# A decoder layer on Trainium2: the root of the FFN's inner layernorm by Newton's method on GpSimd

## The chip, the core and the metric

The kernel runs on one core of a Trainium2 chip. A core has five engines with a queue of instructions each: PE (TensorE, matrix products and transposes), DVE (VectorE), ACT (ScalarE, activation functions), POOL (GpSimd) and SP (SyncE, which issues transfers here). Each works through its queue in order; between engines semaphores say when data is there. The metric is the device time of one execution in microseconds (us).

## The reference

One decoder layer over x of 4 batches x 1024 tokens x 256 features: self-attention with 16 heads, cross-attention over 64 context tokens, and an FFN. Each of the three adds its result to x and begins with a layernorm. What the change touches is the FFN, which has a layernorm of its own between its two products:

```
h = einsum('btd,hd->bth', layernorm(x), absmean(W_fc))   # 256 -> 1024, weights -1, 0, 1
h = gelu(h)
mu  = mean(h);  var = mean((h - mu)**2)                    # over the 1024 values of a token
h = (h - mu) * rsqrt(var + 1e-5) * ln_w + ln_b
x = x + einsum('bth,dh->btd', h, absmean(W_proj))        # 1024 -> 256
```

The change is about `rsqrt(var + 1e-5)` and about when the line that uses it is issued.

## The kernel before

**Stages.** Self-attention of all four batches comes first and takes most of the time, with the cross-attention of each batch but the last woven into it. From about 1098 us on, the FFN of all batches runs, together with what is left of the last batch: its output projection, its cross-attention and the statistics of its last layernorm (the generator `post`, line 554; pieces of it are called the last batch's pieces). The tokens of a batch are worked in two halves of 512 tokens, so the FFN has 8 halves, called 0 to 7. A half has 4 tiles of 128 tokens.

**`widen(i)`** (line 1005) takes half i up. It normalises x into xn, transposes it on PE (L60), copies the transposes out of PSUM as xh on ACT (L279) and the rest xl on DVE (L281). Each tile is then multiplied by `wfc` (16 matmuls into one of the two buffers `ps_wide`); ACT applies Gelu (L1029); DVE takes the statistics of the 1024 values (two `bn_stats`, L1032, and an aggregation into `mvh`, L1033). When all four tiles have their statistics, `ln_rstd` (line 244) makes the reciprocal root of the variances, 128 x 4 values: Sqrt on ACT (L247), reciprocal on DVE (L248, `rsh`), and -mean x root on DVE (L1037, `nmr`). Then the tiles are normalised in place in two steps of two tiles: the even tile on DVE (L1040, needs `rsh`), the odd one on ACT (L1043, needs `nmr`).

**`narrow(i)`** (line 1048) takes half i down. For each of 8 blocks of 128 hidden features it transposes the four tiles (L60, into a bank of `ps_misc`), scales them by `ln_w` as hT on ACT (L1063), takes the rounding rest hl on DVE (L1064), and, two blocks behind, multiplies hl and hT by `wproj` on PE (L57). At the end DVE adds to x (L1082) and SP writes the rows out. `ps_misc` has four banks, which `narrow`, `widen` and the last batch share.

**Tables.** ACT holds one set of functions at a time. Sqrt, Gelu and Exp lie in different sets, so a change from one to another inserts an ACT_TABLE_LOAD in ACT's queue; copies and scalings need none.

**The order** is written out by hand, in pieces. `widen` and `narrow` are generators, and each `yield` ends a piece. Half i's `widen` has its pieces due at places 16 i + `WIDE`, its `narrow` at 16 (i + 1) + `NARROW`:

```
WIDE, NARROW = (-6, -4, 0, 1, 3, 7, 8, 10, 12), (2, 4, 5, 6, 9, 11, 13, 14, 15)
```

The loop after it (lines 1104 to 1130) always steps the piece with the smallest place among the first unfinished `widen` and the first unfinished `narrow`; in two turns of five it steps a piece of the last batch instead, as long as there are any. Of the nine places of `WIDE` the first two make xh and xl, those up to 7 end with the four tiles' matmuls and Gelus, 8 is the root, 10 and 12 are the two steps of normalisation. A condition named `apart` holds back a Gelu or Sqrt piece while the last batch is among its four Exp pieces. PE's instructions are kept in the order in which they are issued (`ordered`, line 56); on the other engines of this stage the framework's scheduler sets the order when the program is built, and it stays fixed from then on.

Of the kernel before, what the change touches and what calls it, by code (L numbers as in the profile page):

```python
# [8 lines left out]

F32 = mybir.dt.float32  # L10
F32R = mybir.dt.float32r
DRAM = bass.MemoryType.DRAM
AF = mybir.ActivationFunctionType
ALU = mybir.AluOpType
# [7 lines left out]
P = 128  # L22
NT = S // P
NG = 4
NU = B * NG
LN_EPS = 1e-5
# [4 lines left out]
def decoder_layer(ctx, tc, a, out):  # L31
# [15 lines left out]
    nc = tc.nc  # L47
# [8 lines left out]
    def matmul(*args, **kwargs):  # L56
        ordered(nc.tensor.matmul(*args, **kwargs))  # L57
# [44 lines left out]
    for name in ("wq", "wk"):  # L102
# [5 lines left out]
        t = const.tile([P, E // P, H, D], F32, name=name)  # L108
# [4 lines left out]
    for name in ("bq", "bk"):  # L113

        t = const.tile([P, 2], F32, name=f"{name}_c")
# [23 lines left out]
    kept_stack = ctx.enter_context(ExitStack())  # L139
    kept_pool = kept_stack.enter_context(tc.tile_pool(name="kept", bufs=1, space=DRAM))  # L140
    x_kept = kept_pool.tile([B * S, E], F32, name="x_kept").rearrange("(t p) d -> p t d", p=P)
# [7 lines left out]
    own = post_pool.tile([P, 4], F32, name="own")  # L149
    sel_x = post_pool.tile([P, 8, SK], F32R, name="sel_x")  # L150

# [3 lines left out]
    nc.gpsimd.memset(nm_s, 0.0)  # L155
    dram = main_stack.enter_context(tc.tile_pool(name="dram", bufs=1, space=DRAM))

# [3 lines left out]
    for i in range(3):  # L161
        t = (const if i else main).tile([P, NT, VW], F32, tag=f"v_sb{i}", name=f"v_sb{i}")
# [22 lines left out]
    def pinned(ins):  # L185

        if state["pinned"]:
            ordered(ins)
# [55 lines left out]
    def ln_rstd(pool, rs, mv):  # L244
        n = mv.shape[1]
        sd = pool.tile([P, n], F32, tag="sd", name="sd", bufs=2)
        nc.scalar.activation(sd, mv[:, :, 1], AF.Sqrt, bias=eps_t[:, 0:1])  # L247
        pinned(nc.vector.reciprocal(out=rs, in_=sd))  # L248

    def ln_normalised(pool, mv, rs, i, t, n):  # L250
        xn = pool.tile([P, n, E], F32, tag="xn", name="xn", bufs=2)
# [100 lines left out]
    def project(b, c):  # L352
# [6 lines left out]
        for side, half in ((0, 0), (1, 0), (1, 1), (0, 1)):  # L359
# [3 lines left out]
            for i0 in range(0, 512, width):  # L363
# [5 lines left out]
                )  # L369
                nc.scalar.activation(hl[:, 0, part].bitcast(F32R), pq, AF.Identity, bias=bias)  # L370
                nc.vector.scalar_tensor_tensor(  # L371
# [7 lines left out]
    def fetch(u):  # L379
# [4 lines left out]
        for pair in range(2):  # L384
            q = main.tile([P, S], F32R, tag="q", name="q", bufs=4)
            k = main.tile([P, S], F32R, tag="k", name="k", bufs=4)
            pairs.append((q, k))
# [66 lines left out]
    def turn_maxima(u, mx):  # L454
# [3 lines left out]
        dst = nm_s[:, :, :, 0:2, :]  # L458
        nc.vector.tensor_copy(dst[:, :, :, :, 0].bitcast(F32R), by_side)
        nc.vector.tensor_tensor(dst[:, :, :, :, 1], by_side, dst[:, :, :, :, 0], ALU.subtract)  # L460
        yield
        views = turned([nm_s[:, n, :, :, :].rearrange("p n a l -> p (n a l)") for n in range(4)])
        mT = main.tile([P, 512], F32R, tag="mT", name="mT", bufs=3)
        for r, v in enumerate(views):
# [447 lines left out]
    for u in range(NU):  # L912
# [27 lines left out]
        for step in range(2 * NT):  # L940
            half, kb = divmod(step, NT)
# [15 lines left out]
            exps = [scores(u, half, kb, 0)]  # L957
# [42 lines left out]
    ffn = ctx.enter_context(tc.tile_pool(name="ffn", bufs=1))  # L1000
    out_view = out.rearrange("(t p) d -> p t d", p=P)
    h_of = {}
    NH = NT // 2

    def widen(i):
        t0 = i * NH
        xh = ffn.tile([P, 2, NH * P], F32R, tag="xh", name="xh", bufs=2)
        xl = ffn.tile([P, 2, NH * P], F32R, tag="xl", name="xl", bufs=2)
        for t in range(0, NH, 2):
            cols = slice(t * P, (t + 2) * P)  # L1010
            xn = ln_normalised(ffn, mv3, rs3, t0 + t, t0 + t, 2)
            ln_transposed(xh[:, :, cols], xn, rest=xl[:, :, cols])
            if t == 0:
                yield ""
        h = ffn.tile([P, NH, HID], F32, tag="h", name="h", bufs=2)
        mv = ffn.tile([P, NH, 2], F32, tag="mvh", name="mvh", bufs=2)
        rs = ffn.tile([P, NH], F32, tag="rsh", name="rsh", bufs=2)
        h_of[i] = h
        for t in range(NH):
            yield "Gelu"  # L1020
            ph = ps["wide"]()
            for half in range(2):
                for k in range(4):
                    c, part = divmod(k, 2)
                    matmul(
                        ph[:, half, :], lhsT=(xl, xh)[part][:, c, t * P : (t + 1) * P],
                        rhs=wfc[:, c, half * 512 : (half + 1) * 512], start=k == 0, stop=k == 3,
                    )
            nc.scalar.activation(h[:, t, :], ph.rearrange("p a f -> p (a f)"), AF.Gelu)  # L1029
            st = ffn.tile([P, 2, 6], F32, tag="bnh", name="bnh", bufs=3)  # L1030
            for half in range(2):
                nc.vector.bn_stats(out=st[:, half, :], in_=h[:, t, half * 512 : (half + 1) * 512])  # L1032
            nc.vector.bn_aggr(out=mv[:, t, :], in_=st)  # L1033
        yield "Sqrt"
        ln_rstd(ffn, rs, mv)
        nmr = ffn.tile([P, NH], F32, tag="nmr", name="nmr", bufs=2)
        nc.vector.scalar_tensor_tensor(nmr, mv[:, :, 0], -1.0, rs, ALU.mult, ALU.mult)  # L1037
        for t in range(0, NH, 2):
            yield ""
            nc.vector.tensor_scalar(  # L1040
                h[:, t, :], h[:, t, :], mv[:, t, 0:1], rs[:, t : t + 1], ALU.subtract, ALU.mult
            )
            nc.scalar.activation(  # L1043
                h[:, t + 1, :], h[:, t + 1, :], AF.Identity, bias=nmr[:, t + 1 : t + 2],
                scale=rs[:, t + 1 : t + 2],
            )
# [57 lines left out]

    WIDE, NARROW = (-6, -4, 0, 1, 3, 7, 8, 10, 12), (2, 4, 5, 6, 9, 11, 13, 14, 15)
    halves = 2 * B
    wides = [Source(widen(i), 16 * i, WIDE) for i in range(halves)]
    narrows = [Source(narrow(i), 16 * (i + 1), NARROW) for i in range(halves)]  # L1110
    exps = turn = 0
    tag = later.tag
    while tag is not None or narrows:
        turn += 1
        if tag is not None and turn % 5 in (0, 2):
            exps += "Exp" in tag
            tag = next(last, None)
            continue
        sources = []
        if wides:  # L1120
            i = halves - len(wides)
            first = len(wides[0].places) <= len(WIDE) - 2
            late_x = i >= 2 * (B - 1) and tag is not None
            full = first and len(narrows) > halves + 1 - i
            apart = exps % NG and tag is not None and wides[0].tag in ("Gelu", "Sqrt")
            if not (late_x or full or apart):
                sources.append(wides[0])
        if narrows and len(narrows) > len(wides):
            sources.append(narrows[0])
        if not sources:  # L1130
            continue
        source = min(sources, key=lambda source: source.places[0])
        source.step()
        if not source:
            (wides if source in wides else narrows).pop(0)
# [58 lines left out]
```

## Time and profile before

| | |
|---|---|
| median of 3 runs | 1352.89 us (1351.7 to 1353.23) |
| the profiled execution | 1356.75 us |
| its span, first to last instruction | 1355.0 us |
| PE busy, share of the span | 1282.8 us, 95% |
| DVE / ACT / POOL busy | 1013.4 / 896.3 / 53.4 us |
| ACT_TABLE_LOADs from 1098 us on | 24 of 1.283 us each (12 ahead of Gelu, 9 ahead of Sqrt, 3 ahead of Exp) |
| Gelu activations L1029 | 32 of 1.025 us |
| normalisations L1040 on DVE / L1043 on ACT | 16 of 0.808 us / 16 of 1.236 us |
| hT L1063 on ACT / hl L1064 on DVE | 64 of 0.687 us / 64 of 0.734 us |

How to read the lines that follow. A line of the timeline has the start in us, the duration in us, the engine, the line of the kernel, the operation, output<-inputs, shapes and the count of instructions that were merged; brackets at its end give how long the engine sat idle before it and what ended that. A line of the waits says who waited for whom, with the total in us, the number of times and the longest. A line of the windows has the stretch and its length, then busy time and count for PE, PEld (weight loads), DVE, ACT and POOL, then PE's granted clock (1.00 is full speed), the DMA share and GB/s. Matmuls are pipelined: they start about 0.23 us apart (128x512) although each is shown longer.

### The profile page before, as it was taken

What the parts mean: (1) busy time and instruction counts of PE and PEld (TensorE: products, weight loads), DVE (VectorE), ACT (ScalarE), POOL (GpSimd) and SP (SyncE); (2) the same over time, 40 slices, a digit from 0 to 9 for tenths busy, and PEclk for the clock granted to TensorE, in tenths of its full rate; (3) what the DMA queues carried; (4) which work ended last, traced back from release to release, by engine and by line L of the source; (5) the groups of instructions that cost most, each with busy time, mean ns of one, the idle gap of its engine ahead of it and who ended that gap; (6) DMA issues with size and microseconds to landing.
All of it is one profiled execution on the core that took longest, in us unless ns stands there. A gap on an engine that the chain in (4) does not pass through costs nothing.

```text
span 1355.0 us, 27659 instructions
## 1 busy us (share of the span) xinstructions
PE 1282.8 (95%) x11000; PEld 719.0 (53%) x11000; DVE 1013.4 (75%) x2130; ACT 896.3 (66%) x1654; POOL 53.4 (4%) x66
## 2 busy tenths in 40 slices
PE   4889999999999999989999999999999999999987
PEld 2344545545545454444545544545455457776777
DVE  5777877867878888778777777778888468585765
ACT  1267686756687767677676676676766756575755
POOL 4000000003010000011000000010000000000000
PEclk9789999999999999999999999999999999999989
DMA  5440412212120202030202111312110010100000
GB/s 165 134 126 29 129 37 90 79 48 63 39 89 1 63 5 60 32 94 25 71 30 66 28 36 53 105 40 87 41 55 1 1 63 1 59 4 32 1 32 31
DMA packets 46576, 72.72 MB, mean 54 GB/s; under 512 B 11536, under 2 KB 28176, under 8 KB 46448
## 3 DMA queue, kind: packets, MB, share of 16 engines
q1 hardware_dynamic: 44976, 68.47, 16.8%
q10 hardware_dynamic: 1328, 2.10, 0.5%
q8 instruction: 87, 1.43, 0.4%
q0 software_dynamic: 144, 0.39, 0.2%
q14 instruction: 41, 0.34, 0.1%
HBM read 46.81 MB, written 24.12 MB: 52 GB/s over the span
## 4 chain that ended last, share of the span: by engine, by line
PE 74%; DVE 16%; ACT 7%; DMA 2%; issue 1%; SPq 0%; DVEq 0%; ACTq 0%
PE ps_ring L57 43%; PE ps_acc L57 15%; PE ps_wide L57 8%; DVE mx L447 7%; PE ps_misc L57 3%; DVE nm L603 3%; ACT exp L909 2%; PE ps_misc L60 2%; PE ps_ring L60 2%; ACT xn L258 1%; DVE bn L241 1%; DMA kept_k<-hl 1%; DMA x<-in_x 1%; ACT ex L636 1%; SPq L63 0%
## 5 line engine op out<-in xcount | busy, mean ns | idle before, releaser
L447 DVE TENSOR_REDUCE mx<-ps_ring 128x1 f32<-128x512 f32 x1024 | 646.9, 682 | 157.5 <-PE ps_ring L57 156.8
L909 ACT ACTIVATE exp<-ps_ring 128x512 f32<-128x512 f32 x1024 | 549.1, 607 | 182.1 <-PE ps_ring L57 178.7
L57 PE MATMUL ps_ring<-q,k 64*128 64x512 f32 x1024 | 280.4, 475 | 6.5 <-ACT exp L909 5.6
L57 PE MATMUL ps_ring<-k,q 64*128 64x512 f32 x1024 | 266.5, 428 | 18.2 <-DMA k<-kept_k 6.6
L57 PE MATMUL ps_acc<-exp,v_sb 128*32 128x512 f32 x2048 | 275.3, 610 | 0.0
L57 PE MATMUL ps_ring<-mT,sel 64*128 64x512 f32 x1024 | 233.4, 402 | 0.4 <-ACT mT L465 0.4
L57 PEld LDWEIGHTS ps_ring<-q,k 64*128 64x128 f32 x1024 | 115.8, 186 | 198.1 <-ACT exp L909 65.7
L57 PEld LDWEIGHTS ps_ring<-k,q 64*128 64x128 f32 x1024 | 127.0, 187 | 100.6 <-ACT exp L909 41.8
L57 PEld LDWEIGHTS ps_ring<-mT,sel 64*128 64x128 f32 x1024 | 108.7, 187 | 6.5 <-ACT mT L465 0.7
L57 PEld LDWEIGHTS ps_acc<-exp,v_sb 128*32 128x32 f32 x2048 | 40.5, 108 | 67.8 <-issue 66.0
L1064 DVE SCALAR_TENSOR_TENSOR hl<-ps_misc,lnw,hT 128x512 fp32r<-128x512 f32 x64 | 46.6, 734 | 20.0 <-ACT hT L1063 19.8
L1032 DVE BATCH_NORM_STATS2 bnh<-h 128x6 f32<-128x512 f32 x64 | 41.1, 680 | 24.7 <-ACT h L1029 24.6
L57 PE MATMUL ps_wide<-wfc,xl 128*128 128x512 f32 x128 | 55.6, 435 | 3.6 <-DVE xl L281 3.1
L1029 ACT ACTIVATE h<-ps_wide 128x1024 f32<-128x1024 f32 x32 | 32.7, 1025 | 36.8 <-PE ps_wide L57 36.7
L57 PE MATMUL ps_wide<-wproj,hl 128*128 128x256 f32 x256 | 46.8, 306 | 10.6 <-DVE hl L1064 10.5
L1063 ACT ACTIVATE hT<-ps_misc,lnw 128x512 fp32r<-128x512 f32 x64 | 42.9, 687 | 15.3 <-PE ps_misc L60 15.2
L57 PE MATMUL ps_wide<-wfc,xh 128*128 128x512 f32 x128 | 52.9, 413 | 0.0
L241 DVE BATCH_NORM_STATS2 bn<-x 128x6 f32<-128x256 f32 x96 | 39.0, 416 | 5.8 <-DMA x<-in_x 4.1
L57 PEld LDWEIGHTS ps_wide<-wproj,hl 128*128 128x128 f32 x256 | 35.3, 194 | 14.3 <-DVE hl L1064 12.6
L57 PE MATMUL ps_wide<-wproj,hT 128*128 128x256 f32 x256 | 42.0, 287 | 0.0
L371 DVE SCALAR_TENSOR_TENSOR hl<-ps_ring,bq_c,hl 128x256 f32<-128x256 f32 (+1 forms) x30 | 14.8, 500 | 31.0 <-ACT hl L370 31.0
L60 PE MATMUL ps_misc<-ident,h 128*128 128x128 f32 x256 | 37.3, 275 | 0.0
(167 smaller groups left out, 1424.0 us busy)
## 6 DMA issues: line engine op xcount, KB each, us to landing
q<-kept_q SPq DMA_DIRECT2D x240, 64.0 KB
k<-kept_k SPq DMA_DIRECT2D x240, 64.0 KB
kept_q<-hl SPq DMA_DIRECT2D x15, 512.0 KB
kept_k<-hl SPq DMA_DIRECT2D x14, 512.0 KB
out<-x SPq DMA_DIRECT2D x16, 256.0 KB
x<-in_x SPq DMA_DIRECT2D x3, 1024.0 KB
x_kept<-x SPq DMA_DIRECT2D x3, 1024.0 KB
x<-x_kept SPq DMA_DIRECT2D x3, 1024.0 KB
```

What stands on the lines that cost most here:

```text
L57: ordered(nc.tensor.matmul(*args, **kwargs))
L60: ordered(nc.tensor.transpose(*args))
L241: pinned(nc.vector.bn_stats(out=st, in_=xs(t)[:, 0, :]))
L258: nc.scalar.activation(xn[:, k, :], xs(t + k)[:, 0, :], AF.Identity, bias=nmr[:, k : k + 1], scale=rs[:, i + k : i + k + 1],)
L371: nc.vector.scalar_tensor_tensor(hl[:, 1, part], pq, bias, hl[:, 0, part], ALU.add, ALU.subtract)
L447: nc.vector.tensor_reduce(mx[:, t, 2 * pair + n : 2 * pair + n + 1, kh], pm, AX.X, ALU.max)
L603: nc.vector.tensor_reduce(nm[:, t, s, :], pm[s].rearrange("p (h k) -> p h k", k=SK), AX.X, ALU.max, negate=True,)
L909: nc.scalar.activation(ex[:, n, :], pe[n], AF.Exp)
L1029: nc.scalar.activation(h[:, t, :], ph.rearrange("p a f -> p (a f)"), AF.Gelu)
L1032: nc.vector.bn_stats(out=st[:, half, :], in_=h[:, t, half * 512 : (half + 1) * 512])
L1063: nc.scalar.activation(hT, pt, AF.Copy, scale=w)
L1064: nc.vector.scalar_tensor_tensor(hl, pt, w, hT.bitcast(F32), ALU.mult, ALU.subtract)
```

## The change

The Sqrt on ACT, the reciprocal and `nmr` on DVE give way to a function `ln_root` that makes both on GpSimd: variance + epsilon, a first guess from the bits of the number, three rounds of Newton's method, and -mean x root, 17 instructions on 128 x 4 values. The root no longer has a piece of its own: it is issued at the end of the piece of the fourth Gelu. The two steps of normalisation move from places 10 and 12 to 12 and 13, one place of `narrow` moves from 13 to 8, the last batch gets 7 turns of 17 instead of 2 of 5, and the condition `apart` names Gelu alone. The layernorms outside `widen` keep `ln_rstd`.

```diff
+    def ln_root(pool, rs, mv):
+        n = mv.shape[1]
+        by = pool.tile([P, 4, n], F32, tag="root", name="root", bufs=2)
+        var, half, t, nmr = (by[:, i, :] for i in range(4))
+        engine = nc.gpsimd
+        engine.tensor_scalar(var, mv[:, :, 1], LN_EPS, None, ALU.add)
+        engine.tensor_scalar(half, var, -0.5, None, ALU.mult)
+        engine.tensor_scalar(
+            rs.bitcast(I32), var.bitcast(I32), -0.5, float(0x5F3759DF), ALU.mult, ALU.add
+        )
+        for _ in range(3):
+            engine.tensor_tensor(t, rs, half, ALU.mult)
+            engine.tensor_tensor(t, t, rs, ALU.mult)
+            engine.tensor_scalar(t, t, 1.5, None, ALU.add)
+            engine.tensor_tensor(rs, rs, t, ALU.mult)
+        engine.tensor_tensor(nmr, mv[:, :, 0], rs, ALU.mult)
+        engine.tensor_scalar(nmr, nmr, -1.0, None, ALU.mult)
+        return nmr
...
-        yield "Sqrt"
-        ln_rstd(ffn, rs, mv)
-        nmr = ffn.tile([P, NH], F32, tag="nmr", name="nmr", bufs=2)
-        nc.vector.scalar_tensor_tensor(nmr, mv[:, :, 0], -1.0, rs, ALU.mult, ALU.mult)
+        nmr = ln_root(ffn, rs, mv)
...
-    WIDE, NARROW = (-6, -4, 0, 1, 3, 7, 8, 10, 12), (2, 4, 5, 6, 9, 11, 13, 14, 15)
+    WIDE, NARROW = (-6, -4, 0, 1, 3, 7, 12, 13), (2, 4, 5, 6, 8, 9, 11, 14, 15)
...
-        if tag is not None and turn % 5 in (0, 2):
+        if tag is not None and turn % 17 in (0, 2, 5, 7, 10, 12, 15):
...
-            apart = exps % NG and tag is not None and wides[0].tag in ("Gelu", "Sqrt")
+            apart = exps % NG and tag is not None and wides[0].tag == "Gelu"
```

## The prediction

> **What bounds the kernel now.** I read the page first. PE is the busiest engine, but a busy PE is not a fast one, so I went on to the stage that the change touches, the FFN (1098 us to the end), and asked for the waits in it, then for the timeline around each of its eight halves (called half 0 to half 7), then for the granted clock in slices of 3 us.
>
> ```profile
> PE 1282.8 (95%) x11000; PEld 719.0 (53%) x11000; DVE 1013.4 (75%) x2130; ACT 896.3 (66%) x1654; POOL 53.4 (4%) x66
> ```
> ```profile
> PEld ps_wide L57 <- DVE hl L1064: 12.6, 9, 3.1
> PE ps_wide L57 <- DVE hl L1064: 10.5, 5, 2.9
> PE ps_wide L57 <- DVE xl L281: 3.1, 2, 2.9
> ```
>
> In these 257 us PE is busy for 231.85. PE's own waits in the timeline are few and long: 2.91 us behind half 0 (at 1121.1), 2.70 in half 3 (1230.8), 1.51 in half 4 (1261.6), 2.70 behind half 5 (1286.5), 2.90 behind half 6 (1310.4), 1.52 behind half 7 (1335.3). So the stage is bound by PE, broken by the turn from one half to the next. Half 6 shows how:
>
> ```profile
> 1307.00 1.28 ACT L247 ACT_TABLE_LOAD   x1
> ...
> 1307.37 0.20 DVE L1033 BATCH_NORM_AGGREGATE mvh<-bnh 128x2 f32<-128x12 f32 x1
> ...
> 1308.84 0.16 DVE L1037 SCALAR_TENSOR_TENSOR nmr<-mvh,rsh 128x4 f32<-128x4 f32 x1
> 1308.92 1.53 DVE L1040 TENSOR_SCALAR h<-h,mvh,rsh 128x1024 f32<-128x1024 f32 x2
> 1309.04 2.37 ACT L1043 ACTIVATE h<-h,nmr,rsh 128x1024 f32<-128x1024 f32 x2
> ...
> 1312.52 0.74 DVE L1064 SCALAR_TENSOR_TENSOR hl<-ps_misc,lnw,hT 128x512 fp32r<-128x512 f32 x1
> 1313.32 1.22 PE L57 MATMUL ps_wide<-wproj,hl 128*128 128x256 f32 x4 [2.90 <-DVE hl L1064]
> ```
>
> See the last line: PE has waited 2.90 us for an hl that DVE makes late, because ACT had the table load and two normalisations in front of that hl's hT. See also that the root costs little here: the statistics end at 1307.57 and nmr stands at 1309.00, 1.43 us later (1.54 in half 1). The table load ran mostly before the statistics were there. What comes after a long wait costs as much as the wait:
>
> ```profile
> 1311.00:1314.00 3.00, 0.68 (x3) 0.69 (x4) 1.40 (x3) 2.75 (x4) 0.00 (x0) 0.76 0.00 0
> 1314.00:1317.00 3.00, 3.00 (x12) 2.61 (x12) 1.29 (x2) 0.00 (x0) 0.00 (x0) 0.50 0.00 0
> 1317.00:1320.00 3.00, 3.00 (x10) 2.36 (x9) 0.10 (x1) 1.03 (x1) 0.00 (x0) 0.60 0.52 175
> ```
>
> The column before the DMA share is PE's granted clock. Summing 3 us times what is missing to 1: about 3.4 us lost here, and about 1.7 us each after the waits of halves 0, 3 and 5. After 1.51 and 1.52 us nothing is lost.
>
> **The change, part by part.**
>
> *Removed.* The built program's order shows 15 table loads fewer (43 to 28): 15 x 1.283 = 19.2 us of ACT, with 8 x 0.30 (sd) of ACT and 8 x (0.175 + 0.157) of DVE. ACT is busy 157 of 257 us, so this is worth something only where ACT's queue holds up PE: halves 0, 3, 4 and 5.
>
> *Added: the chain on GpSimd.* 17 instructions on 128x4, each but one waiting for the one before by a semaphore (15 of them up to rs, all for nmr). POOL does nothing in this stage today, and the trace has no such chain. The nearest rows are its copies, 0.237 us for 128x64, 0.401 for 128x256, 0.625 for 128x512: 0.875 ns an element and 0.18 us for 4 elements. Ahead of that comes the hop:
>
> ```profile
> 10.82 0.32 POOL L134 MEMSET vx<- 64x32 f32 x1
> 11.19 0.53 POOL L146 MEMSET nm_x<- 128x512 f32 x1
> ```
> ```profile
> 301.38 0.42 DVE L549 SCALAR_TENSOR_TENSOR bo<-ps_ring,bo 128x256 f32<-128x256 f32 x1 [1.28 <-PE ps_ring L57]
> 301.89 1.28 POOL L291 TENSOR_TENSOR x<-x,bo 128x512 f32<-128x512 f32 x1 [27.75 <-DVE bo L549]
> ```
>
> L146 waits for L134 and starts 0.05 us after it; L291 starts 0.09 after the DVE result. So I take 0.18 + 0.07 = **0.25 us a link**: rs after 15 x 0.25 = 3.75 us, nmr after 4.25 us, against 1.45 now. Lower bound: eight copies that do not wait start 0.179 apart, less 60 elements is 0.13. Upper bound: L134 to L146, 0.37. The value is nearest to the copies. All chains together move the end by about 1 us for each 0.01 us of a link (0.15 to 0.17 in each of six halves).
>
> *Moved.* The normalisations go from places 10 and 12 to 12 and 13, so three pieces of the other half (0.44 transposes + 0.95 matmuls = 1.39 us each) lie behind the last Gelu before them. On PE that is the same work as before up to the next half's first matmul. But DVE's two L1040 and ACT's two L1043 keep their place in queues that are served in order, and whatever stands behind them waits for the root. Take T as the end of the half's last wfc matmul (1138.43 in half 1, 1280.32 in half 5, 1304.26 in half 6, 1329.86 in half 7); the statistics end at T + 3.3 in halves 1, 6 and 7 of the trace, so rs would stand at T + 7.1 and an L1043 start at T + 7.6. PE's work from T to the next half's wfc is 6.95 in halves 5 and 6 (three pieces 4.17, transposes 0.88, two piece ends 1.9).
>
> - Half 0. rs at 1117.55 + 3.75 = 1121.3, L1040 1.53, xl 0.69: next wfc at 1123.6, now 1124.0. Gain 0.4, and the clock loss (1.7) perhaps not: the wait becomes 2.3, between the 1.52 that cost nothing and the 2.70 that did. Half of it: **-1.25**.
> - Half 1. PE has no wait here today, because the query projections stand ahead of the normalisations on ACT (below). In the new order ACT has h, q, hT, h, q. With h at T + 7.6: 1.23 + 0.68 + 0.68 + 1.24 + 0.68 puts the second q at T + 12.1. PE's work up to the matmuls that read it: three pieces 4.17, transposes 0.87, projections 3.68 = 8.7. A new wait of 3.4 and the clock after it, at least 1.7: **+5.1**.
> - Half 2. xh and the first ao stand ahead of the normalisations, and ACT's load behind them goes: 0.
> - Half 3. DVE's L1040 now stands ahead of the two reductions L603 that free PSUM banks (4 in the pool): four stalls of PE, in sum 2.2. Later two Gelus stand together, without the loads at 1224.9 and 1229.2: 1.1, and the wait falls to 2.0, so no clock loss, 1.7. **-0.6**.
> - Half 4. attx no longer stands behind xl: **-0.75**.
> - Half 5. xh stands ahead of h on ACT; rs T + 7.1, L1040, xl: wfc at T + 9.4, now T + 10.7 and 0.6 of slow clock behind it. Gain 1.9, less half of 1.7 for a wait of 2.45: **-1.05**.
> - Half 6. xh stands behind both h: T + 7.6 + 2.37 + 0.57 + 0.69 + hops = T + 11.3, now T + 10.9; clock loss behind it 1.7 to 3.4, now 1.9: **+0.6**.
> - Half 7. Nothing lies behind it. The transposes need all four tiles: T + 7.6 + 2.37 = T + 10.0, now T + 7.95: 2.05, and PE has then idled 3.9 us, so about 1 of clock: **+3.05**.
>
> ```profile
> 1142.72 0.67 ACT L299 ACTIVATE q<-ps_misc,xbq 128x512 f32<-128x512 f32 x1
> ...
> 1143.29 1.23 ACT L1043 ACTIVATE h<-h,nmr,rsh 128x1024 f32<-128x1024 f32 x1
> 1144.42 0.68 ACT L299 ACTIVATE q<-ps_misc,xbq 128x512 f32<-128x512 f32 x1
> ```
>
> On the clock, the Trainium skill (TensorE: Matmul & The Clock Gate, "HAM oscillation") has it that only idle gaps over about 3.4 us throttle. The rows above disagree: 2.70 and 2.90 us were enough. By the page halves 0 and 5 would be 1.7 us better in sum. The skill also says (GPSIMD Engine Reference, "Key points") that GpSimd shares its SBUF interfaces with VectorE and contends with instructions that read two SBUF inputs; the adds L291 (0.684 us, 16 in this stage) are such. No run here shows it; by it, two adds in half 1 would make its wait an estimated 1.4 us longer.
>
> The ratio 7 of 17 for 2 of 5 (0.412 for 0.400) brings the last batch's pieces forward by one turn in 85; in the built order they shift by one piece at most. I set it at 0, between -1 and +1.4 (one piece of 1.39).
>
> Sum: -1.25 + 5.1 - 0.6 - 0.75 - 1.05 + 0.6 + 3.05 = **+5.1 us**. The profiled execution took 1356.75 (span 1355.0 and 1.75 around it), so 1361.9 for it; it lies 3.86 above the median of the runs, so 1352.89 + 5.1 = **1358.0**.
>
> **The rivals.**
> - *The chain is short* (faster). At 0.17 a link it ends 1.36 us sooner in each half: 7.8 off the sum, and the waits of halves 1 and 7 fall to 2.0 and 2.6, 2.7 of clock less: -5.4, **1347.5**. It decides from 0.21 a link down. For it: unhindered copies start 0.179 apart. Against: every link waits.
> - *The chain is long*, DVE in its way or two-input operations dearer (128x512 adds take 1.275, copies 0.625). At 0.31: +6 and 2 of clock: **1366**.
> - *It cancels*: the gains of halves 0, 3, 4 and 5 (3.65) come, and half 1 is saved because the last batch's pieces fall otherwise: about **1353**.
>
> **How the numbers follow.** Forecast (link 0.22 to 0.28, 1356 to 1362): 0.40. Long: 0.17. Cancels: 0.11. Short: 0.32. Within 0.2% (2.7 us) is no change, about what a measurement of this kernel can tell. Slower 0.57, same 0.11, faster 0.32. For 8 in 10 the links go from 0.14 (-10.5) to 0.32 (+14): 1342 to 1367; of the forecast alone 1354 to 1362.
>
> **What would show it.** Right: POOL links at 0.25 us, nmr 4.2 us behind mvh; a PE wait of about 3.4 us before the kx matmuls of half 1 and 3.9 before the last twelve transposes; waits of 2.0 to 2.5 behind halves 0 and 5; clock at 0.5 after the long ones. Wrong: links under 0.21, or ACT reaching half 1's second q by T + 9.

## The result and the profile after

The changed kernel takes 1378.8 us (1374.65 to 1379.52, 5 runs) beside 1352.89 of the kernel before: 1.018 times as long [1.0167, 1.0192]. The forecast was +5.1 us and 1358.0; +25.9 came, above the upper end of the range, 1367. The direction was right, the size was not. The profiled execution took 1379.52 us (span 1377.7); lines of the code are numbered 1 to 23 higher than before (L57 is now L58, L1040 is L1060, L1043 is L1063, L1064 is L1084, L281 is L304, L299 is L322, L603 is L626).

First the busy line of the page of the changed kernel:

```profile
PE 1291.6 (94%) x11000; PEld 724.8 (53%) x11000; DVE 1012.0 (73%) x2114; ACT 875.0 (64%) x1631; POOL 85.3 (6%) x202
```

Then its waits in the FFN stage (who <- for whom: us in total, times, longest):

```profile
ACT h L1063 <- POOL root L270: 32.0, 8, 5.6
...
DVE h L1060 <- POOL rsh L268: 22.7, 8, 3.3
...
PE ps_wide L58 <- DVE xl L304: 11.1, 4, 5.1
...
PE ps_misc L58 <- ACT q L322: 4.1, 2, 2.6
PE ps_wide L58 <- DVE hl L1084: 4.1, 4, 2.1
```

ACT is busy for 21 us less, as the table loads went, and PE for 9 us more at the same 11000 matmuls, which is a slower clock. The first two wait lines are new: eight times, once in each half, ACT and DVE stand idle at the head of their queues until GpSimd has the root, 32.0 and 22.7 us in all. In the kernel before, ACT's normalisations waited for `nmr` 1.7 us in all, and DVE for the Sqrt 2.8. PE's waits have moved from hl (10.5 us before, 4.1 now) to xl (3.1 before, 11.1 now) and q (none before). Half 6 in the timeline shows how:

```profile
1323.74 0.20 DVE L1056 BATCH_NORM_AGGREGATE mvh<-bnh 128x2 f32<-128x12 f32 x1
...
1328.13 0.20 POOL L268 TENSOR_TENSOR rsh<-rsh,root 128x4 f32<-128x4 f32 x1
1328.37 1.53 DVE L1060 TENSOR_SCALAR h<-h,mvh,rsh 128x1024 f32<-128x1024 f32 x2 [2.84 <-POOL rsh L268]
...
1328.70 0.57 POOL L270 TENSOR_SCALAR root<-root 128x4 f32<-128x4 f32 x1
1329.30 2.37 ACT L1063 ACTIVATE h<-h,root,rsh 128x1024 f32<-128x1024 f32 x2 [4.56 <-POOL root L270]
...
1332.17 1.29 DVE L304 TENSOR_TENSOR xl<-ps_misc,xh 128x512 fp32r<-128x512 f32 x2 [1.67 <-ACT xh L302]
...
1332.92 0.79 PE L58 MATMUL ps_wide<-wfc,xl 128*128 128x512 f32 x1 [5.06 <-DVE xl L304]
```

The statistics end at 1323.94; rs stands at 1328.33 and nmr at 1329.27, 5.33 us later (1.43 before; on average over the halves 5.4, and 2.35 before, as other work lies between its instructions in some halves). DVE has been idle for 2.84 and ACT for 4.56 us. Then come xh on ACT, xl on DVE, and PE, which has waited 5.06 us for it where the kernel before waited 2.90 for an hl. In the three windows from 1329 to 1338 the granted clock is 0.81, 0.50 and 0.55.

**Where the time went.** The stage begins 2.15 us sooner in this execution (first Gelu at 1105.09, 1107.24 before) and lasts 24.85 us longer from there. PE's waits over 1 us sum to 26.0 (15.3 before, +10.7), and what the granted clock lacks to 1, times the time for which it lacks it, from 1098 us to the end of the span, sums to 21.7 (9.3 before, +12.5). Some 1 us of that increase lies inside waits or behind the last matmul, where it costs nothing. Together 22 to 23 of the 24.85: about half waits, half clock.

A table by half says where. A half is counted from the start of its first Gelu to that of the next (half 7 to the end of the span). The forecast's half 3 was made of +2.2 for stalls ahead of half 4's first Gelu and -2.8 for what comes behind it; the -2.8 is therefore counted in half 4. The columns to the right belong to experiments that are told below.

| half | before | changed | difference | forecast | e1, old root | e16, pinned | e9, fused |
|---|---|---|---|---|---|---|---|
| 0 | 19.95 | 20.42 | +0.47 | -1.25 | 17.04 | 20.67 | 16.08 |
| 1 | 29.88 | 40.48 | +10.60 | +5.1 | 32.59 | 32.52 | 30.22 |
| 2 | 38.73 | 41.22 | +2.49 | 0 | 39.15 | 41.22 | 39.10 |
| 3 | 30.41 | 38.41 | +8.00 | +2.2 | 32.79 | 32.52 | 33.64 |
| 4 | 42.46 | 40.08 | -2.38 | -3.55 | 39.77 | 40.08 | 38.10 |
| 5 | 24.90 | 24.30 | -0.60 | -1.05 | 24.80 | 24.44 | 23.30 |
| 6 | 25.27 | 26.73 | +1.46 | +0.6 | 21.65 | 26.30 | 19.48 |
| 7 | 36.16 | 40.97 | +4.81 | +3.05 | 35.03 | 40.75 | 36.84 |
| sum | 247.76 | 272.61 | +24.85 | +5.1 | 242.82 | 258.50 | 236.76 |

Halves 1 and 3 hold 11.3 of the 19.75 us that the forecast missed.

### The profile page after: what moved, and what is told of

It reads as the page before. It is cut to its first block, busy times and chain, and to the rows that moved or that the text cites. A ratio compares the mean times of both kernels' runs of the same rounds, so it can differ in the third digit from the quotient of the medians.

```text
span 1377.7 us, 27775 instructions
## 1 busy us (share of the span) xinstructions
PE 1291.6 (94%) x11000; PEld 724.8 (53%) x11000; DVE 1012.0 (73%) x2114; ACT 875.0 (64%) x1631; POOL 85.3 (6%) x202
## 3 DMA queue, kind: packets, MB, share of 16 engines
q1 hardware_dynamic: 44976, 68.47, 16.5%
q8 instruction: 87, 1.43, 0.4%
## 4 chain that ended last, share of the span: by engine, by line
PE 71%; DVE 15%; ACT 7%; issue 2%; POOL 2%; DMA 2%; SPq 0%; POOLq 0%; DVEq 0%; ACTq 0%
PE ps_ring L58 43%; PE ps_acc L58 15%; PE ps_wide L58 7%; DVE mx L470 7%; ACT exp L932 2%; PE ps_misc L58 2%; PE ps_ring L61 2%; DVE nm L626 2%; PE ps_misc L61 2%; DVE bnh L1055 1%; DMA x<-in_x 1%; ACT xn L281 1%; ACT h L1052 1%; DVE hl L1084 1%; DVE bn L242 1%
## 5 line engine op out<-in xcount | busy, mean ns | idle before, releaser
L58 PE MATMUL ps_ring<-q,k 64*128 64x512 f32 x1024 | 279.4, 474 | 6.7 <-ACT exp L932 5.8
L58 PE MATMUL ps_ring<-k,q 64*128 64x512 f32 x1024 | 265.7, 428 | 17.2 <-DMA k<-kept_k 6.5
L58 PE MATMUL ps_acc<-exp,v_sb 128*32 128x512 f32 x2048 | 274.4, 608 | 0.0
L58 PE MATMUL ps_ring<-mT,sel 64*128 64x512 f32 x1024 | 232.4, 401 | 0.2 <-ACT mT L488 0.2
L58 PEld LDWEIGHTS ps_ring<-q,k 64*128 64x128 f32 x1024 | 115.3, 185 | 196.9 <-ACT exp L932 67.2
L58 PEld LDWEIGHTS ps_ring<-k,q 64*128 64x128 f32 x1024 | 126.5, 187 | 100.2 <-ACT exp L932 42.2
L58 PEld LDWEIGHTS ps_ring<-mT,sel 64*128 64x128 f32 x1024 | 108.1, 187 | 6.4 <-ACT mT L488 0.7
L58 PEld LDWEIGHTS ps_acc<-exp,v_sb 128*32 128x32 f32 x2048 | 40.5, 108 | 67.2 <-issue 65.4
L58 PE MATMUL ps_wide<-wfc,xl 128*128 128x512 f32 x128 | 57.3, 448 | 11.2 <-DVE xl L304 11.1
L1084 DVE SCALAR_TENSOR_TENSOR hl<-ps_misc,lnw,hT 128x512 fp32r<-128x512 f32 x64 | 46.6, 735 | 26.4 <-ACT hT L1083 26.2
L1055 DVE BATCH_NORM_STATS2 bnh<-h 128x6 f32<-128x512 f32 x64 | 41.0, 681 | 24.9 <-ACT h L1052 24.4
L58 PE MATMUL ps_wide<-wfc,xh 128*128 128x512 f32 x128 | 54.2, 423 | 0.0
L58 PE MATMUL ps_wide<-wproj,hl 128*128 128x256 f32 x256 | 47.8, 311 | 4.2 <-DVE hl L1084 4.1
L58 PE MATMUL ps_wide<-wproj,hT 128*128 128x256 f32 x256 | 42.4, 289 | 0.0
L58 PEld LDWEIGHTS ps_wide<-wproj,hl 128*128 128x128 f32 x256 | 36.3, 198 | 8.4 <-DVE hl L1084 6.0
L1063 ACT ACTIVATE h<-h,root,rsh 128x1024 f32<-128x1024 f32 x16 | 19.1, 1234 | 32.0 <-POOL root L270 32.0
```

The source lines that it names most:

```text
L1063: nc.scalar.activation(h[:, t + 1, :], h[:, t + 1, :], AF.Identity, bias=nmr[:, t + 1 : t + 2], scale=rs[:, t + 1 : t + 2],)
L1084: nc.vector.scalar_tensor_tensor(hl, pt, w, hT.bitcast(F32), ALU.mult, ALU.subtract)
```

## The experiments

**Theory A**: the root on GpSimd is late, DVE and ACT stand behind it, PE waits and then loses clock. **Theory B**: the new places and the new ratio put the pieces into a worse order, whatever makes the root. All kernels are edits of the changed kernel or of the one before; "places" includes the place of the root and the condition `apart`, and a link is one instruction of the root's chain. The median of the kernel before lay between 1353.2 and 1354.3 in these series; each ratio is to the runs of its own series.

| kernel | us | ratio to before | DVE / ACT idle for the root, us |
|---|---|---|---|
| before | 1352.9 | | 2.8 / 1.7 |
| changed | 1378.8 | 1.018 [1.0167, 1.0192] | 22.7 / 32.0 |
| e1 old root, changed places and ratio | 1346.17 | 0.9951 [0.9935, 0.9967] | 3.3 / 1.0 |
| e2 GpSimd root, old places and ratio | 1381.84 | 1.0211 [1.0196, 1.0226] | 24.5 / 33.2 |
| e3 changed, ratio back | 1384.89 | 1.0232 [1.0217, 1.0247] | 24.9 / 36.0 |
| e4 changed, the 17 instructions on DVE | 1362.27 | 1.0057 [1.0041, 1.0074] | 0 / 10.8 |
| e6_rounds_1, 9 links | 1358.05 | 1.0033 [1.0022, 1.0045] | 11.1 / 20.3 |
| e6_rounds_6, 29 links | 1398.62 | 1.033 [1.0305, 1.0354] | 45.3 / 54.1 |
| e8 changed, idle Sqrt | 1384.76 | 1.0228 [1.0209, 1.0246] | 27.5 / 27.3 |
| e9 fused root on DVE, changed places and ratio | 1342.26 | 0.9917 [0.9900, 0.9933] | 0 / 10.4 |
| e10 before, changed ratio | 1363.33 | 1.0064 [1.0049, 1.0080] | 1.6 / 1.9 |
| e11 old root, changed places, old ratio | 1345.68 | 0.9933 [0.9920, 0.9946] | 2.5 / 0.5 |
| e12 fused root, old places and ratio | 1349.24 | 0.9961 [0.9946, 0.9976] | 0 / 13.8 |
| e13 changed, root in two parts | 1401.14 | 1.0339 [1.0314, 1.0363] | 36.8 / 58.1 |
| e14 fused root, changed places, old ratio | 1342.88 | 0.9917 [0.9904, 0.9929] | 0 / 8.5 |
| e15 changed, two places later | 1379.72 | 1.0189 [1.0170, 1.0208] | 22.7 / 33.4 |
| e16 changed, queues pinned | 1364.2 | 1.0076 [1.0061, 1.0091] | 17.1 / 22.3 |

(The profiled executions of e1 and e9 are some 5 us above their medians; in e9 the stage begins 2 us later than in the kernel before.)

### The root or the order: e1, e2, e3, e4

e1 puts the old root into the changed order.

```diff
-        nmr = ln_root(ffn, rs, mv)
+        ln_rstd(ffn, rs, mv)
+        nmr = ffn.tile([P, NH], F32, tag="nmr", name="nmr", bufs=2)
+        nc.vector.scalar_tensor_tensor(nmr, mv[:, :, 0], -1.0, rs, ALU.mult, ALU.mult)
```

> The changed kernel with its root made the old way (Sqrt on ACT, reciprocal and nmr on DVE) at the changed place; places, ratio and condition as changed. Theory A (the changed kernel is slow because its root stands 5.2 us behind the statistics instead of 1.45, with DVE's and ACT's queues behind it, and PE's clock falls after each longer wait): 1350 to 1360 us, waits behind halves 1, 6 and 7 shorter by 2 us and more. Theory B (the changed places and ratio put the pieces in a worse order, whatever makes the root): 1370 us and more, and the waits of 2.06 us (hl, at 1133.8) and 2.29 us (attx, at 1197.7) that the prediction did not have are still there.

1346.17 us: below theory A's band, and faster than both kernels. In the same order, the root alone makes the difference between 1346 and 1379. The 2.3 us wait for attx (the last batch's attention result) is still there (at 1190.3), and the one for hl is 1.66 us, so these two belong to the order, as theory B had it, but they are small. Half 6 of e1, in the timeline:

```profile
1306.64 0.20 DVE L1056 BATCH_NORM_AGGREGATE mvh<-bnh 128x2 f32<-128x12 f32 x1
...
1308.11 0.16 DVE L1059 SCALAR_TENSOR_TENSOR nmr<-mvh,rsh 128x4 f32<-128x4 f32 x1
```

nmr stands 1.43 us behind the statistics (2.1 on average over the halves), and DVE idles 0.44 us on the way, in front of the reciprocal. e2 is the other half of the pair: `ln_root` in the kernel before, at the old root's place, with everything else as before.

```diff
         yield "Sqrt"
-        ln_rstd(ffn, rs, mv)
-        nmr = ffn.tile([P, NH], F32, tag="nmr", name="nmr", bufs=2)
-        nc.vector.scalar_tensor_tensor(nmr, mv[:, :, 0], -1.0, rs, ALU.mult, ALU.mult)
+        nmr = ln_root(ffn, rs, mv)
```

> The kernel before with the root on GpSimd alone; places, ratio and condition as before. Theory A: slower than the changed kernel or like it, 1372 to 1395 us, since the normalisations come two places sooner after a root that is 3.7 us later. Theory B: 1350 to 1362 us, as the order is the old one. The links of the chain should stand 0.28 to 0.31 us apart, as in the changed kernel.

1381.84 us, inside theory A's bounds. Root alone: +28; places and ratio alone: -8 (e1); both: +26. e3 takes the ratio back.

```diff
-        if tag is not None and turn % 17 in (0, 2, 5, 7, 10, 12, 15):
+        if tag is not None and turn % 5 in (0, 2):
```

> The changed kernel with the last batch's turns put back from 7 of 17 to 2 of 5. Theory A: 1373 to 1384 us, within 5 us of the changed kernel, as the root's chain stays. Theory B in the form that the ratio is what costs: under 1366 us, and the 2.06 us wait at 1133.8 and the 2.29 us wait at 1197.7 gone.

1384.89 us, 0.9 above the band: the ratio isn't what costs, and it is worth 6 us here. e4 makes the same root on DVE.

```diff
-        engine = nc.gpsimd
+        engine = nc.vector
```

> The changed kernel with the same 17 instructions on VectorE in place of GpSimd. Small DVE operations take 0.16 to 0.20 us in the trace, so rs stands some 2.8 us and nmr 3.2 us behind the statistics, 2 us sooner than on GpSimd, and DVE is busy 3.2 us more in each half. Theory A: 1358 to 1370 us. Theory B: 1372 us and more. If the table loads that are gone were worth anything, under 1353 us.

1362.27 us, as theory A said, but not for the reason given: in the trace the instruction that reads the mean for nmr ends 5.6 us behind the statistics on average in e4, and 4.8 in the changed kernel. On DVE the chain is **later** and the kernel 16.5 us faster. What differs is the last column of the table: in e4 DVE never stands idle for the root, since other instructions lie between the links. So theory A was narrowed: lateness alone is not what costs; it costs where DVE and ACT stand idle in front of the root.

### How the time goes with the chain: e6, e8

One and six rounds in place of three; with one the root is only rough.

```diff
-        for _ in range(3):
+        for _ in range(1):
```

> The changed kernel with one round of Newton's method in place of three (the root is then only rough): 9 links on GpSimd in place of 17, nmr some 2.3 us sooner. The old root at the same places gave 1346.2 us, the changed kernel 1378.8, for a root 3.7 us later: 8.7 us of time for each us of root. If that is a straight line, 1357 to 1361 us. If most of it is the clock, lost only after waits over 2 us or so, the time falls faster at first: 1348 to 1356.

> The changed kernel with six rounds in place of three: 29 links, nmr some 3.5 us later in each of eight halves. On the straight line of 8.7 us for each us of root: 1405 to 1413 us. If other work comes into the gap of a longer chain, less: 1390 to 1403.

1358.05 and 1398.62 us. 8 links fewer (nmr 3.0 us behind the statistics in place of 5.3) give 20.75 us, 2.6 a link; 12 more cost 19.8, 1.65 a link. The first is the straight line (1357 to 1361), the second (two runs) came below it, in the lower of the two bands, but not for its reason, which was that other work comes into the gap: the idle time for the root grows by more a link in the second step (DVE 11.1, 22.7, 45.3 us and ACT 20.3, 32.0, 54.1). PE's waits over 1 us grow with the links too, 15.8, 26.0, 37.7 us in all. What flattens is the clock: what it lacks sums to 8.0, 21.7 and 25.6 us.

e8 brings the table loads back and leaves the chain.

```diff
         nmr = ln_root(ffn, rs, mv)
+        sd = ffn.tile([P, NH], F32, tag="sd", name="sd", bufs=2)
+        nc.scalar.activation(sd, mv[:, :, 1], AF.Sqrt, bias=eps_t[:, 0:1])
```

> The changed kernel with the old Sqrt put back on ACT at the end of ln_root, its result unused, so that the table loads come back and the chain on GpSimd stays. If the loads lie beside other work: 1376 to 1384 us. If the loads bind where ACT is waited for (15 of 1.283 us, 19.2 in all): 1387 to 1398 us.

1384.76 us, just above the lower band: 6 us for 19.2 us of loads and the eight Sqrt. In this kernel what the change takes off ACT is worth about a third of its length.

### A short root on DVE: e9, e12, e14

e9 shortens the root and makes it on DVE; two of the three instructions of a round do two steps at once.

```diff
-        engine = nc.gpsimd
+        engine = nc.vector
         engine.tensor_scalar(var, mv[:, :, 1], LN_EPS, None, ALU.add)
-        engine.tensor_scalar(half, var, -0.5, None, ALU.mult)
         engine.tensor_scalar(
             rs.bitcast(I32), var.bitcast(I32), -0.5, float(0x5F3759DF), ALU.mult, ALU.add
         )
...
+        for _ in range(2):
+            engine.scalar_tensor_tensor(t, rs, -0.5, rs, ALU.mult, ALU.mult)
+            engine.tensor_tensor(t, t, var, ALU.mult)
+            engine.scalar_tensor_tensor(rs, t, 1.5, rs, ALU.add, ALU.mult)
+        engine.scalar_tensor_tensor(nmr, mv[:, :, 0], -1.0, rs, ALU.mult, ALU.mult)
```

> The changed kernel with the root on VectorE in 8 instructions up to rs and 1 for nmr: two rounds of three instructions each, two of them with both steps fused. At 0.20 us from link to link on DVE (as in the kernel with all 17 there) rs stands 1.6 us and nmr 1.8 us behind the statistics, with no table loads. If only the length of the chain counts: 1345 to 1351 us (the old root at these places, 1.45 us, gave 1346.2). If the loads that go are worth something as well: 1338 to 1344. If DVE being busy with the chain costs as much again: 1352 to 1358.

1342.26 us, the band in which the loads that go are worth something as well: 0.9917 times the kernel before and some 36 us under the changed kernel. But nmr doesn't stand after 1.8 us. Half 6 in the timeline:

```profile
1303.07 0.20 DVE L1053 BATCH_NORM_AGGREGATE mvh<-bnh 128x2 f32<-128x12 f32 x1
...
1306.19 0.68 DVE L301 TENSOR_TENSOR xl<-ps_misc,xh 128x512 fp32r<-128x512 f32 x1
...
1306.98 0.16 DVE L267 SCALAR_TENSOR_TENSOR root<-mvh,rsh 128x4 f32<-128x4 f32 x1
1307.03 0.39 PE L58 MATMUL ps_wide<-wfc,xl 128*128 128x512 f32 x1
1307.06 1.53 DVE L1057 TENSOR_SCALAR h<-h,mvh,rsh 128x1024 f32<-128x1024 f32 x2
```

nmr ends at 1307.14, 3.87 us behind the statistics: later than in the kernel before (1.43) and later than with one round on GpSimd (3.0); on average over the halves it is 3.7. Yet PE has its xl in time and doesn't wait, as an hl (at 1304.11) and both xl (the first at 1305.51) were done between the links and stand ahead of the normalisation. This is the plainest row for the narrowed theory. The half takes 19.48 us, 25.27 before. But idle time isn't the whole price: e4 and e9 stand idle for the root alike (0 and 10.8, 0 and 10.4 us), yet e4, with eight links more and nmr 6.4 us behind the statistics on average, is 20 us slower. That the extra links take DVE's time and make the root later is the likely reason; it wasn't taken apart.

e12 puts this root into the kernel before, at the old places and ratio, and e14 keeps the changed places with the old ratio:

```diff
         yield "Sqrt"
-        ln_rstd(ffn, rs, mv)
-        nmr = ffn.tile([P, NH], F32, tag="nmr", name="nmr", bufs=2)
-        nc.vector.scalar_tensor_tensor(nmr, mv[:, :, 0], -1.0, rs, ALU.mult, ALU.mult)
+        nmr = ln_root(ffn, rs, mv)
```

> The kernel before, order and all, with the fused root on VectorE (8 instructions to rs, 1 for nmr). In the changed order it gave 1342.3 us where the old root gave 1346.2. If the two gains add: 1348 to 1351 us. If a short root needs no later place, so that the changed order is worth nothing to it: 1341 to 1345. If the old order's places come too soon for 1.8 us: 1353 and more.

1349.24 us: the gains of the short root (-5) and of the changed places (-8 in e1, -8.6 in e11) about add; e9 has both (-11.5).

```diff
-        if tag is not None and turn % 17 in (0, 2, 5, 7, 10, 12, 15):
+        if tag is not None and turn % 5 in (0, 2):
```

> The changed kernel with the fused root on VectorE and the last batch's turns back at 2 of 5. With the old root the ratio made no difference at these places (1345.7 us with 2 of 5, 1346.2 with 7 of 17), with the long GpSimd root it cost 6.1 us to take it back. If the ratio's worth is a chance of what meets a wait, and the short root leaves few waits: 1339 to 1345 us, like 1342.3 with 7 of 17.

1342.88 us: the ratio doesn't matter here.

### The ratio and the places by themselves: e10, e11

e10 is the kernel before with the ratio; e11 is e1 with the old ratio (the diff of e14).

```diff
-        if tag is not None and turn % 5 in (0, 2):
+        if tag is not None and turn % 17 in (0, 2, 5, 7, 10, 12, 15):
```

> The kernel before with 7 of 17 turns for the last batch in place of 2 of 5, and nothing else. The prediction set this at 0 (-1 to +1.4). Taking the ratio back in the changed kernel cost 6.1 us; if that is the ratio's own worth, this stands at 1346 to 1349 us; if it is a chance of which pieces meet the long root, within 3 us of the kernel before.

1363.33 us, +9 and outside both bands: neither a gain of its own nor nothing. PE has ten waits over 1 us in the stage, 21.3 us in all, where the kernel before has 15.3.

> The kernel before with the changed places and condition, the old root at the end of the fourth Gelu's piece, and 2 turns of 5. Places and ratio together gave 1346.2 us with the old root. If the places carry that gain: 1345 to 1349. If the ratio carries it: 1351 to 1356.

1345.68 us: the places carry the gain. The ratio by itself was worth +9 (e10), -6 (e3 against the changed kernel), +0.5 (e1 against e11) and -0.6 us (e9 against e14). No worth of its own shows in these four; that it only shifts which piece meets a wait is an argument that no trace was read for.

### Where it stands in the queues: e13, e15, e16

e13 makes the root of tiles 0 and 1 as soon as they have their statistics, and that of tiles 2 and 3 after the fourth tile, with four `root` buffers.

```diff
             nc.vector.bn_aggr(out=mv[:, t, :], in_=st)
+            if t % 2 == 1:
+                nmrs.append(ln_root(ffn, rs[:, t - 1 : t + 1], mv[:, t - 1 : t + 1, :]))
-        nmr = ln_root(ffn, rs, mv)
```

> The changed kernel with the root on GpSimd in two parts: tiles 0 and 1 as soon as their statistics stand, tiles 2 and 3 after the fourth. 34 instructions a half in place of 17, the last rs and nmr as late as before, but the first normalisation on DVE and the first on ACT no longer wait for it. If what hurts is that the root is late for the first of the two steps in the queues: 1358 to 1370 us. If the second step (one place behind the first) then waits as long: 1374 to 1380. If POOL being busy hurts: 1380 and more.

1401.14 us, the slowest of all, in the third band but not for its reason, which was that POOL is busy (in half 0 it idles 3.8 us between the two chains). The timeline of half 0:

```profile
1113.27 0.81 DVE L1062 TENSOR_SCALAR h<-h,mvh,rsh 128x1024 f32<-128x1024 f32 x1 [3.57 <-POOL rsh L268]
1114.00 1.28 DVE L1056 BATCH_NORM_STATS2 bnh<-h 128x6 f32<-128x512 f32 x2
```

The first normalisation is issued eleven places after the second tile, and stands in DVE's queue ahead of the third tile's statistics: there the scheduler put it. DVE idles 3.57 us at its head. An earlier root became an earlier wait, and twice as many of them (15 in the trace). So the place in the hand-written order is not the place in DVE's queue. e15 and e16 take this apart: e15 changes places alone, e16 queues alone.

```diff
-    WIDE, NARROW = (-6, -4, 0, 1, 3, 7, 12, 13), (2, 4, 5, 6, 8, 9, 11, 14, 15)
+    WIDE, NARROW = (-6, -4, 0, 1, 3, 7, 14, 15), (2, 4, 5, 6, 8, 9, 11, 14, 15)
```

> The changed kernel with the two steps of normalisation at places 14 and 15 in place of 12 and 13. The built order shows PE's instructions moved by a piece in four places and ACT's normalisations where they were but for one row. If the places set how long DVE and ACT stand behind the root: ACT's 32 us of waiting for it falls by some 2 us a half, and the time to 1355 to 1368 us. If the queues' order is set by the framework's scheduler and not by the places: 1374 to 1384 us, ACT's waiting 29 to 33 us.

1379.72 us, and 33.4 us of ACT's waiting, just above the 33 of the second case: two places more change nothing. e16 keeps the two normalisations, hT, hl and the evictions q in program order:

```diff
-            nc.scalar.activation(hT, pt, AF.Copy, scale=w)
+            ordered(nc.scalar.activation(hT, pt, AF.Copy, scale=w))
```

and so for hl (L1084), L1060, L1063 and the eviction q (L322, the copy of the query projection out of PSUM).

> The changed kernel with both normalisations, hT, hl and the query projections' evictions kept in program order on ACT and DVE. In half 1 both evictions q then stand ahead of both normalisations on ACT, which the prediction had as the cause of half 1's loss. If that order is what costs in half 1: its two waits for q (2.55 and 1.58 us) are gone and the time is 1366 to 1374 us. If the loss is the root's lateness wherever it is met: 1374 us or more, with a wait elsewhere in its place.

1364.2 us, 2 us under the first band: 14.6 us back, at the same chain. The table by half shows that all of it lies in halves 1 (-8.0) and 3 (-5.9), which are now as long as with the old root (32.59 and 32.79 in e1); the other halves stay as in the changed kernel. First half 1 of the changed kernel, in the timeline:

```profile
1144.78 0.68 DVE L314 TENSOR_TENSOR x<-x,yrow 128x512 f32<-128x512 f32 x1
...
1144.93 0.59 POOL L265 TENSOR_TENSOR root<-rsh,root 128x4 f32<-128x4 f32 x1
...
1149.65 1.24 ACT L1063 ACTIVATE h<-h,root,rsh 128x1024 f32<-128x1024 f32 x1 [5.64 <-POOL root L270]
...
1150.80 0.67 ACT L322 ACTIVATE q<-ps_misc,xbq 128x512 f32<-128x512 f32 x1
...
1151.52 0.70 PE L58 MATMUL ps_misc<-kx,q 64*128 64x256 f32 x4 [2.55 <-ACT q L322]
...
1151.93 1.23 ACT L1063 ACTIVATE h<-h,root,rsh 128x1024 f32<-128x1024 f32 x1
...
1153.07 0.68 ACT L322 ACTIVATE q<-ps_misc,xbq 128x512 f32<-128x512 f32 x1
...
1153.80 1.22 PE L58 MATMUL ps_misc<-kx,q 64*128 64x256 f32 x4 [1.58 <-ACT q L322]
```

And half 1 of e16:

```profile
1141.64 0.68 DVE L314 TENSOR_TENSOR x<-x,xbo 128x512 f32<-128x512 f32 x1
1141.68 1.30 POOL L266 TENSOR_TENSOR root<-root,rsh 128x4 f32<-128x4 f32 x1
1142.24 0.69 DVE L314 TENSOR_TENSOR x<-x,yrow 128x512 f32<-128x512 f32 x1
...
1142.74 0.69 ACT L322 ACTIVATE q<-ps_misc,xbq 128x512 f32<-128x512 f32 x1 [1.88 <-PE ps_misc L58]
...
1145.84 0.69 ACT L322 ACTIVATE q<-ps_misc,xbq 128x512 f32<-128x512 f32 x1 [1.83 <-PE ps_misc L58]
...
1146.83 2.38 ACT L1063 ACTIVATE h<-h,root,rsh 128x1024 f32<-128x1024 f32 x2 [0.30 <-POOL root L270]
```

In the changed kernel ACT idles 5.64 us in front of h with q behind it, and PE waits twice for q, 2.55 and 1.58 us. In e16 both q stand ahead of h, ACT fills its time with them, waits 0.30 us for the root, and PE's waits for q are gone. The root is even later here (its chain takes 6.3 us).

## Why the prediction came out as it did

**Right, and shown.** The sign, and half 1's mechanism: that h, q, hT, h, q stand in this order on ACT and that PE then waits for q is what the trace has, and e16, which changes that order, takes 8.0 us out of the half. The wait of 3.4 us was 2.55 + 1.58 = 4.13. In half 7 the waits ahead of the last twelve transposes are 2.36 + 0.96 + 0.69 = 4.01 us (forecast 3.9). The removed loads are worth a part only (e8).

**The link, mis-sized.** 0.25 us was forecast; in half 6 the seventeenth link starts 4.61 us after the first, 0.288 apart, and the last takes 0.57. nmr stands at 5.33 us (forecast 4.25), in half 1 at 5.97. By the forecast's own slope (1 us for 0.01) this is worth +3.8 and would have given about 1362, still in the forecast's own range. It is the lesser part. (The 1.45 us that the prediction had for the root of the kernel before are those of halves 6 and 7; the average of the eight is 2.35.)

**The step that failed: the clock, priced by the length of a wait.** From the rows of the kernel before (nothing lost after 1.51 and 1.52 us, 1.7 or 3.4 us after 2.70 and 2.90) the prediction took it that a wait of 2.0 to 2.5 us costs half a loss or none, and it gave the stalls of half 3 none at all. Its clock terms, gains and losses together, come to under 1 us, as far as its sums tell them apart; measured are +12.5.

Half 3 shows it best. What the prediction had there as "four stalls of PE, in sum 2.2", without a clock loss, came as one wait of 2.07 us for `nm` (the reduction L626), from 1229.79 to 1231.86, and the windows from there on are these (changed kernel; the clock is the column ahead of the DMA share):

```profile
1230.00:1233.00 3.00, 1.14 (x6) 0.97 (x8) 2.40 (x4) 2.40 (x3) 0.56 (x1) 0.82 0.00 0
1233.00:1236.00 3.00, 2.55 (x12) 1.38 (x8) 2.29 (x4) 0.55 (x1) 0.00 (x0) 0.50 0.00 0
1236.00:1239.00 3.00, 3.00 (x14) 2.20 (x14) 2.15 (x4) 1.17 (x2) 0.00 (x0) 0.50 0.00 0
1239.00:1242.00 3.00, 3.00 (x16) 2.26 (x13) 2.30 (x5) 0.00 (x0) 0.00 (x0) 0.50 0.00 0
```

3 x (0.18 + 0.50 + 0.50 + 0.50) = 5.0 us of clock, where the prediction had none. Its "wait falls to 2.0, so no clock loss" is another wait: that for hl, 2.70 us at 1230.8 in the kernel before, behind half 4's first Gelu. It is gone altogether (half 4 has no wait over 1 us now), and that 2.0 and 2.07 are alike is chance. Against the old root in the same order (e1) half 3 is 5.6 us longer; the other 2.4 of its +8.0 come with the order, and go again in half 4 (e1 has -2.7 there). In half 1 the clock behind the waits cost 3.4 us (windows 1152 to 1161 at 0.73, 0.50 and 0.63), twice the 1.7 that the prediction gave as the least, and a wait of 2.06 us for hl at 1135.9, which it didn't have, took 1.7 of clock with it (with the old root it is 1.66 us and takes none). In half 7 the clock took 3.4, forecast 1; in half 5, where half a loss was forecast, a wait of 2.68 us took none. Why waits of like length cost so differently is told in the last section: what counts is how long PE idles within one slice of 3.41 us.

**What it had wrong in its picture.** The prediction treated the two places as cover for the root: carried on along its own slope (+5.1 us at 4.25 us of root, 0.15 us of root for each us of time), it held 3.5 us of root to be free. At the new places the old root (1.43 us in half 6, 2.1 on average) gives 1346 and nine links (3.0 us) give 1358, so on the line between them the kernel before's 1353 is reached at 2.3 to 2.6 us, an estimate, as the two differ in the table loads too; and from nine links to seventeen a us of root costs 9 us, where the prediction's slope was 6.7. The cover is some 2.5 us, and e15 shows that later places don't add to it: two more change nothing. What stands ahead of the normalisations in DVE's and ACT's queues is set by the scheduler, and in e13, e15 and the changed kernel their reader of the root comes up before the root is there. The prediction did say that the two "keep their place in queues that are served in order, and whatever stands behind them waits"; it then priced that by PE's waits in the trace of before, half by half, and put gains of 5.85 us into halves 0, 4 and 5 (counted as in the table), of which halves 4 and 5 brought 2.98 (half 4 no more than with the old root in e1) and half 0 turned into a small loss.

**Half 2 (+2.5, forecast 0).** The 2.3 us wait for attx is there with the old root too (e1), and in e16; it comes with the changed order and wasn't seen. It isn't the whole: with it half 2 is only 0.4 us longer in e1, and the other 2.1 us, which e16 keeps, weren't taken apart.

**The ratio, set at 0.** Between kernels that differ in nothing else it moved the time by +9, -6, +0.5 and -0.6 us; -1 to +1.4 was much too narrow; that the mean of the four is about 0.7 us is no merit of the forecast.

**The rival that the chain is short** fails by its own bound (0.21 a link). GpSimd's contention with VectorE, which the prediction could weigh only by the Trainium skill (GPSIMD Engine Reference, "Key points": GpSimd shares its SBUF interfaces with VectorE and contends with instructions of two SBUF inputs), is in the trace: L259 and L265 of half 1 took 0.56 and 0.59 us beside adds L314, whose two inputs lie in SBUF, 0.23 and 0.20 in half 6. The chain of half 1 is 0.71 us longer for it (5.32 from first to last start, 4.61 in half 6), half of the 1.4 that was estimated.

What stays open: a GpSimd root with xl pinned ahead of the normalisations too (as e9's queue has it) wasn't tried, so whether the losses of halves 0, 6 and 7, which e16 leaves, can be covered on GpSimd isn't known. What made e10 slow wasn't taken apart.

## What to carry to other kernels

Moving a short serial step to an idle engine saved nothing here, as its result is read by an instruction at the head of a busy engine's queue: look at the idle time of the reading engines (here 55 us of DVE and ACT for 26 us of time), and in the built order for what stands behind the reader. The idle time points to the place; it is no price by itself (e4 and e9). With a wait of PE of 2 us or so count 1.7 us of clock or more: here the clock took about as much as the waits. A root made on DVE itself, ready later than the old one (3.87 against 1.43 us in half 6) but with other work between its links, was faster than both kernels. And where two versions differ in order only, a few us either way, up to 9 here, can come from the order alone; undo the order and the operation separately before believing either.

## What the runs showed of the hardware

- A chain of dependent GpSimd instructions on 128x4 runs at 0.288 us a link (0.19 to 0.23 us each), on 128x2 (e13) at about the same, 0.284; on DVE the same instructions take 0.16 us and start 0.20 us apart when nothing lies between.
- GpSimd was held up beside DVE's adds L314, whose two inputs both lie in SBUF: one 128x4 multiplication took 1.30 us under two of them back to back in e16, 0.20 alone. Beside hl L1084 and xl L304, which have one of their two inputs in PSUM, links of the changed kernel took 0.19 to 0.23 us as ever. The last link took 0.57 us in place of the 0.23 of the same kind (L260) in every half, where the first L1060 passes to the second; the link ahead of it, L269, beside the first L1060 alone, took 0.20. What makes that difference isn't shown.
- The clock doesn't follow from a wait's length. After waits of 1.70 us (e3), 1.81 (e6_rounds_1), 2.06 and 2.07 (changed) it fell to 0.5 to 0.6; after 1.66 (e1), 2.68 (changed, half 5), 2.68 (e16) and 2.76 (e6_rounds_1) it stayed at 1.0.
- It follows from PE's idle time in slices of time. In the FFN stage of the 17 traces the granted clock fell to 0.5 for 81 stretches that end before the span does: 42 last 3.41 us, 36 last 6.83 and 3 last 10.24, and all those of one trace begin on one grid of 3.41 us. Cut the stage by that grid: of the slices at full clock in which PE idled 1.88 us or more, all 76 were followed by a slice at 0.5; of the 1049 in which it idled under 1.27 us, none; between, 5 of 44. The wait of 2.07 us lies in one slice, that of 2.68 us in half 5 is split over two (1.84 and 0.84 us idle):

```profile
1228.47:1231.89 3.42, 1.35 (x10) 0.81 (x9) 2.22 (x4) 1.29 (x2) 1.60 (x7) 1.00 0.00 0
1231.89:1235.30 3.41, 2.96 (x12) 1.98 (x13) 2.23 (x4) 1.66 (x2) 0.00 (x0) 0.50 0.00 0
...
1303.57:1306.99 3.42, 1.58 (x14) 1.38 (x12) 1.35 (x2) 0.42 (x1) 2.22 (x10) 1.00 0.00 0
1306.99:1310.40 3.41, 2.57 (x11) 2.11 (x12) 3.25 (x8) 2.83 (x4) 0.00 (x0) 1.00 0.23 77
1310.40:1313.81 3.41, 3.41 (x21) 2.87 (x20) 3.41 (x9) 2.57 (x4) 0.00 (x0) 1.00 0.24 82
```

The Trainium skill (TensorE: Matmul & The Clock Gate, "What's actually happening") has a window of 3413 ns that runs freely, and the length of the slices agrees. The same page's rule that only gaps over about 3.4 us throttle doesn't hold here.
